# Turning normalised rows through memory and blocks on VectorE, and a written order for the last 13 attention steps

## The chip, the cores and the metric

The kernel runs on one core of one Trainium2 chip. The metric is the time of one execution on the device in microseconds (us), lower is better. It is the median of three runs, beside one execution that the hardware profiler recorded. All arithmetic is in float32.

## The reference, cut to what matters

An image x of 4 x 16 x 16 x 1024 passes two layers, three blocks in all, each of which adds to x: a convolution-like attention with relative positions (four heads), a causal attention (16 heads of 64, four sequences of 256 tokens), and a mixture of eight experts, of which each token takes those whose gate is at least 0.1.

```python
x = x + _L0_conv_ref(_gn(x), ...)                  # group norm, then lambda layer
t = _to_tokens(x)                                  # 4 x 256 tokens of 1024
t = t + _L1_attn_ref(_ln_t(t), W_attn, b_attn, W_proj, b_proj)
t = t + _L1_ffn_ref(_ln_t(t), gate_w, gate_b, expert_w, expert_b)

def _ln_t(v, eps=1e-5):
    m = jnp.mean(v, axis=-1, keepdims=True)
    s = jnp.var(v, axis=-1, keepdims=True)
    return (v - m) / jnp.sqrt(s + eps)
```

Both layer norms `_ln_t` are places of the change, and so is the end of `_L1_attn_ref`.

## The kernel before

**Shapes.** The 1024 tokens are eight tiles of 128 rows (NT = 8), the 1024 channels eight chunks of 128 (NC = 8). Image b holds tiles 2b and 2b + 1. A matrix product on PE wants the channels on the partitions, so that each tile of normalised rows has to be turned before it is used.

**Who sets the order.** Outside the blocks marked `tc.manual_schedule()` a scheduler orders the instructions of each engine when the kernel is built: by the order of the source and by its own costs, it takes what it holds to be ready. Each engine then works in that fixed order, SP's queue of transfers included. In a `manual_schedule` block the block's own instructions keep the order of the source on the engines named (without names, on all of them).

**End of the first block (lines 419 to 453).** For each tile, in the order 1, 3, 5, 7, 0, 2, 4, 6: two products `pc` (line 342) that VectorE adds into `s0`, four pairs of products `py` (443) that VectorE adds to x, and `layer_norm` (155 to 171): statistics on VectorE, the root on ACT, the normalised row on ACT (166), eight turnings on PE into PSUM (170), two copies on ACT into `ln1` (171). GpSimd then adds the output bias of the attention to x (452), and SP stores the tile in memory as `x_rows` (453).

**Attention.** `project_v` (499) makes V by seven products of blocks instead of eight (Strassen's way, as everywhere here): `sums_of_A` (149) and `sums_of_B` (479) are VectorE's sums for it. Queries and keys of a pair of heads come from seven units `project_qk(pair, n)` (532), each one product of half width. Then 32 steps follow, one for each pair of heads and image, the last eight with the pairs 6 and 7 in turn (673). A step's `scores` (573) are a product into the one PSUM tile `sc`, scale and mask on VectorE (593), row maxima (605), four exponentials on ACT (607), reciprocals (614) and four multiplications on GpSimd (617). The rows go out to memory (623) and come back in four reads (627), so that `turned` (630) has only to turn blocks of 32 x 32 on VectorE (632). `values` (638) of a step come three steps later (`lag`). `units` (675 to 681) says which units stand in which step, and `out_at` (682) which pieces of the output projection `project_out` (658) do: (tile, half of the channels), 16 matmuls by the profile's count. All of this is left to the scheduler. At step 27 SP loads x back from `x_rows`, eight tiles of 512 KB (694 to 697). The weights of the projection, two halves of 2 MB, are asked for with the first piece (660).

**Start of the experts (lines 708 to 1029).** The other ten pieces of the projection are cut into 20 halves. `after` (1003) places each tile's four stages behind numbered halves: `normalise` (853), `gate` (874), `place` (905), `enter` (941). `normalise` makes the row on VectorE (863), turns it on PE (845) with a copy on ACT (849) and one on VectorE (851), brings the row into quarters on ACT (867) and stores it in `rows` (871), from which the experts' rows are later gathered. Ahead of it SP is asked for the weights and the bias of expert 0 (984, 985).

Of the kernel before, what the change touches and what calls it, by code (L numbers as in the profile page):

```python
# [32 lines left out]
F32 = mybir.dt.float32  # L33
I32 = mybir.dt.int32
AF = mybir.ActivationFunctionType
# [32 lines left out]
def kernel(  # L68
# [86 lines left out]
    def layer_norm(ln, t, dst):  # L155
# [8 lines left out]
        less = small.tile([P, 1], F32, tag="ln_less", name=f"ln1_less{t}")  # L164
        nc.vector.scalar_tensor_tensor(less, mv[:, 0:1], -1.0, rstd, ALU.mult, ALU.mult)
        nc.scalar.activation(ln, xs[t], AF.Identity, bias=less, scale=rstd)  # L166
        for j in range(2):
            pt = tr(f"ln1_pt{t}_{j}")
            for c in range(4):
                nc.tensor.transpose(pt[:, ts(c, P)], ln[:, (4 * j + c) * P : (4 * j + c + 1) * P], ident)  # L170
            nc.scalar.copy(dst[:, 4 * j : 4 * j + 4, ts(t, P)], pt.rearrange("p (c n) -> p c n", c=4))


    with ExitStack() as layer0:
# [253 lines left out]
        ln1 = big_tile(1, "ln1")  # L428
        ln_rows = wpool.tile([P, 4, C], F32, tag="w", name="ln_rows")
        bp = ln_rows[:, 3, :]  # L430
        nc.gpsimd.dma_start(bp, b_proj.partition_broadcast(P))
        for i, (b, nt) in enumerate(tiles):
            if i == 0:
                content(b, nt)
            if i + 1 < NT:
                content(*tiles[i + 1])
            t = 2 * b + nt
            for hp in range(2):
                py = mm(f"py{t}_{hp}")
                for hl in range(2):  # L440
                    bh = b * HEADS0 + 2 * hp + hl
                    for mh in range(2):
                        nc.tensor.matmul(  # L443
                            py[:, ts(hl, M)],
                            s0[:, mh, ts(nt, S2), :, bh].rearrange("p i j -> p (i j)"),
                            v_T[:, mh, ts(b, M)],
                            start=(mh == 0),
                            stop=(mh == 1),
                        )
                nc.vector.tensor_add(xs[t][:, ts(hp, HALF)], xs[t][:, ts(hp, HALF)], py)  # L450
            layer_norm(ln_rows[:, i % 3, :], t, ln1)
            nc.gpsimd.tensor_add(xs[t], xs[t], bp)  # L452
            nc.sync.dma_start(x_rows[ts(t, P), :], xs[t])
# [3 lines left out]
    with ExitStack() as attention:  # L457
# [41 lines left out]
        def project_v(r):  # L499
# [3 lines left out]
            sums_of_A(*a, s1, s2, s4)  # L503
# [7 lines left out]
            for t in range(4):  # L511
                c11, c12, c21, c22 = homes(t)
                nc.scalar.copy(c22, one(t, 1, a11, b11))
                nc.vector.tensor_add(c11, one(t, 2, a12, b21), c22)
# [3 lines left out]
            for t in range(4):  # L518
                nc.scalar.copy(homes(t)[1], one(t, 3, s4, b22))
# [11 lines left out]

        def project_qk(pair, n):

            g, at = pair // 2, (pair % 2) * P
            if n == 1:
# [3 lines left out]
                S[pair] = s_pool.tile([P, 3, NC // 2, P], F32, tag="S", name=f"S_qk{pair}")  # L539
            a = [w_qk[g][:, 4 * j : 4 * j + 4, i * M + at : i * M + at + P] for i in range(2) for j in range(2)]  # L540
            a11, a12, s3, a22 = a
            s1, s2, s4 = (S[pair][:, i, :, :] for i in range(3))
            if n == 1:
                sums_of_A(*a, s1, s2, s4)
# [28 lines left out]
        def scores(pair, b):  # L573
# [29 lines left out]
            for qt in range(2):  # L603
                cols = slice(qt * P, qt * P + (qt + 1) * P)
                nc.vector.tensor_reduce(top[:, qt, :], s[:, :, cols], AX.X, ALU.max, negate=True)
                for h in range(2):
# [6 lines left out]
                    )  # L613
            nc.vector.reciprocal(total, total)  # L614
# [43 lines left out]
        def project_out(t, j, halfway=lambda: None):  # L658
            if not w_p:
                w_p.extend(w_tile(f"w_p{j}", W_projT[:, ts(j, HALF)]) for j in range(2))  # L660
            po = mm(f"po{t}_{j}")
            for c in range(NC):
                nc.tensor.matmul(po, y_T[:, c, ts(t, P)], w_p[j][:, c, :], start=(c == 0), stop=(c == NC - 1))  # L663
                if c == NC // 2 - 1:
                    halfway()
# [13 lines left out]
        units[22].remove((6, 5))  # L679
        units[23] = [(6, 5)]  # L680
# [668 lines left out]
```

## Time and profile before

| | |
|---|---|
| three runs | 1278.26, 1278.86 (median), 1281.36 us |
| profiled execution | 1278.4 us |
| its span on the core | 1276.6 us |
| mean granted clock of PE | 0.991 |
| first block with its layer norm, to the first product of V | 0 to 282.6 us |
| V, queries and keys, attention steps | 282.6 to 690.5 us |
| rest of the projection, gates and lists | 690.5 to 786 us |
| experts | 786 to 1276.6 us |

PE is TensorE's matmuls, PEld its weight loads, DVE is VectorE, ACT is ScalarE, POOL is GpSimd, and SP is the engine that issues most transfers. Lines such as L170 are lines of the kernel; a group's line gives what is written and read, the shape, the count, then the busy time in us and the mean of one in ns, and behind the second bar the idle time before it and what ended that. An instruction whose time overlaps its neighbour's shows more than it costs: of PE the distance from start to start is what counts. The granted clock of PE is given as a share of full speed. The profile counts two matmul instructions for each matmul of the source.

### The profile page before, as it was taken

The numbers are of one execution on the slowest core, as the hardware profiler recorded it, in microseconds if no ns is written. First come the engines' busy times: TensorE is split into PE (matmuls) and PEld (weight loads), VectorE is DVE, ScalarE is ACT, GpSimd is POOL, SyncE is SP. The second block draws the span as 40 slices with busy tenths as digits, with TensorE's granted clock in tenths as the row PEclk, the third lists the DMA queues.
The fourth block names the chain that finished last, engine by engine and source line by source line (L and its number), as shares of the span: only waits on it lengthen the run. The fifth ranks groups of instructions, "written<-read, shape, count | busy, mean of one in ns | idle before, by whom it ended". The sixth has DMA issues, their size and how long they took to land.

```text
span 1276.6 us, 12809 instructions
## 1 busy us (share of the span) xinstructions
PE 1248.8 (98%) x4646; PEld 657.0 (51%) x4646; DVE 694.6 (54%) x1297; ACT 221.6 (17%) x520; POOL 350.0 (27%) x423
## 2 busy tenths in 40 slices
PE   9999999999999999999889998999999999999997
PEld 5444895788884444444434544444344434433443
DVE  5784220566322666665545754755656665665642
ACT  3300111231000222222221322011111110111110
POOL 0000051230000222222210011554644544363520
PEclk9999999999999999999889998999999999999999
DMA  9020022612202535353744415274658375557442
GB/s 353 7 66 2 16 63 70 232 65 99 67 1 66 153 102 163 108 168 99 246 137 154 174 50 210 71 232 89 185 150 232 90 231 154 141 118 210 99 82 51
DMA packets 83605, 159.76 MB, mean 125 GB/s; under 512 B 8368, under 2 KB 39104, under 8 KB 83536
## 3 DMA queue, kind: packets, MB, share of 16 engines
q1 hardware_dynamic: 70704, 119.49, 27.3%
q0 software_dynamic: 12832, 39.39, 14.0%
q8 instruction: 38, 0.62, 0.2%
q14 instruction: 31, 0.25, 0.1%
HBM read 109.30 MB, written 45.35 MB: 121 GB/s over the span
## 4 chain that ended last, share of the span: by engine, by line
PE 75%; issue 13%; POOL 5%; DVE 3%; DMA 3%; ACT 0%; SPq 0%; POOLq 0%; ACTq 0%; DVEq 0%
PE p L1120 29%; PE po L663 7%; PE pq L259 7%; PE pv L492 7%; POOL s_q L617 5%; PE left L1162 3%; PE pT L378 3%; PE pqk L492 3%; PE py L443 2%; PE pk L321 2%; PE pc L342 2%; PE pv L403 2%; PE rest L1176 2%; PE last_pe L1274 1%; DMA s_rows<-s_q 1%
## 5 line engine op out<-in xcount | busy, mean ns | idle before, releaser
L735 POOL DMA_INDIRECT w_e_xg<-rows,gather x146 | 155.2, 1063 | 67.5 <-issue 41.7
L1120 PE MATMUL p<-w_e,A 128*128 128x512 f32 x368 | 163.2, 593 | 1.8 <-DVE slot L981 1.8
L617 POOL TENSOR_TENSOR s_q<-s_q,total 128x128 f32<-128x128 f32 (+1 forms) x128 | 65.3, 541 | 301.9 <-DVE total L614 301.9
L663 PE MATMUL po<-w_p,y_T 128*128 128x512 f32 x256 | 119.5, 613 | 0.0
L1120 PEld LDWEIGHTS p<-w_e,A 128*128 128x128 f32 x368 | 69.6, 190 | 90.4 <-issue 89.9
L1120 PE MATMUL p<-T,S 128*128 128x512 f32 x256 | 112.7, 593 | 0.0
L1126 ACT ACTIVATE y<-y,slot 128x512 f32<-128x512 f32 x64 | 46.0, 721 | 336.3 <-DVE y L1134 183.9
L763 POOL DMA_INDIRECT out_dram<-y,add x32 | 57.4, 1794 | 171.0 <-ACT y L1126 110.1
L259 PE MATMUL pq<-w_q,xn 128*128 128x512 f32 x224 | 99.6, 596 | 1.4 <-DVE q_s L263 1.1
L607 ACT ACTIVATE s_q<-s,top 128x256 f32<-128x256 f32 (+1 forms) x128 | 56.6, 443 | 182.6 <-issue 143.1
L492 PE MATMUL pqk<-ln,w_qk 128*128 128x512 f32 x192 | 86.0, 596 | 0.0
L1120 PEld LDWEIGHTS p<-T,S 128*128 128x128 f32 x256 | 48.6, 190 | 60.8 <-issue 60.7
L663 PEld LDWEIGHTS po<-w_p,y_T 128*128 128x128 f32 x256 | 47.5, 195 | 52.1 <-issue 51.9
L745 DVE STREAM_TRANSPOSE A<-w_e_xg 128x1024 f32<-128x1024 f32 x32 | 39.6, 1238 | 59.8 <-DMA w_e_xg<-rows,gather 56.6
L259 PEld LDWEIGHTS pq<-w_q,xn 128*128 128x128 f32 x224 | 41.8, 190 | 51.8 <-issue 47.4
L492 PE MATMUL pqk<-T,S_qk 128*128 128x512 f32 x128 | 58.3, 598 | 0.0
L492 PEld LDWEIGHTS pqk<-ln,w_qk 128*128 128x128 f32 x192 | 35.8, 190 | 42.7 <-issue 41.5
L1120 PE MATMUL p<-w_e,S 128*128 128x512 f32 x128 | 57.5, 592 | 0.0
L1120 PE MATMUL p<-T,A 128*128 128x512 f32 x128 | 57.5, 592 | 0.0
L492 PE MATMUL pv<-w_v,ln 128*128 128x256 f32 x192 | 43.4, 379 | 0.0
L1162 PE MATMUL left<-w_e,one 128*32 128x512 f32 x312 | 41.8, 593 | 0.0
L452 POOL TENSOR_TENSOR x_at<-x_at,ln_rows 128x1024 f32<-128x1024 f32 x8 | 19.4, 2429 | 76.6 <-ACT ln_rows L166 76.6
(265 smaller groups left out, 1781.0 us busy)
## 6 DMA issues: line engine op xcount, KB each, us to landing
w_e<-in_expert_w_dram SPq DMA_DIRECT2D x16, 2048.0 KB, 12.2
s_rows<-s_q SPq DMA_DIRECT2D x32, 384.0 KB, 2.5
s_rows<-s_rows SPq DMA_DIRECT2D x128, 96.0 KB, 2.4
w_qk<-in_W_attnT_dram SPq DMA_DIRECT2D x8, 1024.0 KB, 6.1
xn<-in_xT_dram SPq DMA_DIRECT2D x8, 512.0 KB, 5.8
x_at<-in_x_dram SPq DMA_DIRECT2D x8, 512.0 KB, 8.5
w_v<-in_W_attnT_dram SPq DMA_DIRECT2D x2, 2048.0 KB
x_rows<-x_at SPq DMA_DIRECT2D x8, 512.0 KB, 2.7
```

Of the source, the lines that this page charges most:

```text
L259: nc.tensor.matmul(pq, xn[:, c, ts(t, P)], w_q[kc][:, c, :], start=(c == 0), stop=(c == NC - 1))
L378: nc.tensor.matmul(out_T[:, g, :, :], window[:, kc, :, :].rearrange("p i j -> p (i j)"), q0[:, kc, first : first + n_i, nj, :], start=(kc ...
L492: nc.tensor.matmul(bank, stationary(c), moving(c), start=(c == 0), stop=(c == NC // 2 - 1))
L607: nc.scalar.activation(blocks(h, qt), s[:, h, cols].rearrange("p (b f i) -> p b f i", f=Q, i=32), AF.Exp, bias=top[:, qt, h : h + 1], accu ...
L617: nc.gpsimd.tensor_mul(blocks(h, qt), blocks(h, qt), total[:, qt, h : h + 1].unsqueeze(2).unsqueeze(3).to_broadcast([P, 1 + qt, Q, 32]),)
L663: nc.tensor.matmul(po, y_T[:, c, ts(t, P)], w_p[j][:, c, :], start=(c == 0), stop=(c == NC - 1))
L735: nc.gpsimd.indirect_dma_start(out=row[:, g, :], out_offset=None, in_=table[: (TOK - P) * Q, :] if e in SHORT else table, in_offset=bass.I ...
L745: nc.vector.transpose(row_T[:, :, :slots].rearrange("p c (g j) -> p g c j", j=32), row[:, : slots // 32, :].rearrange("p g (c i) -> p g c ...
L763: nc.gpsimd.indirect_dma_start(out=out[: TOK - P, :] if e in SHORT else out, out_offset=bass.IndirectOffsetOnAxis(ap=add[:slots, e, k : k ...
L1120: nc.tensor.matmul(bank, a[:, c, :], b[:, c, :], start=(c == 0), stop=(c == NC // 2 - 1))
L1126: nc.scalar.mul(y[i][:, ts(j, HALF)], y[i][:, ts(j, HALF)], slot[:, e, 1, 2 * pair + i : 2 * pair + i + 1])
L1162: nc.tensor.matmul(bank[ts(i, 32), :], stationary, w[of][j][:, c, :], start=(c == 0), stop=(c == NC - 1))
```

## The change

The change has four parts.

1. In the first layer norm ACT writes the normalised row by quarters, SP stores it in a scratch tile in memory and reads it back in four transfers, each into 32 partitions, and VectorE turns the 32 x 32 blocks. PE's turnings and ACT's copies go. SP's own order in this loop is that of the source, and GpSimd stores x. `sums_of_A` of V stands behind the last layer norm on VectorE, and the first products of V take the tiles in the order 1, 3, 0, 2.
2. Steps 22 to 34 of the attention (34 because the values lag by three) stand in a `manual_schedule` for all engines. Units come ahead of or behind a step's values and scores; in steps with a piece of the projection these stand before the last of its eight matmuls. The sums of pair 7 move to step 22. `scores` is cut in two: what ends with the exponentials, and `scored`, which has the rest from the reciprocal on.
3. x is loaded from GpSimd's queue, two tiles in each of the steps 28 to 31. The weights of the projection are asked for in steps 22 and 28, and the pieces' order becomes (0,0), (1,0), (0,1), (1,1), (2,0), (2,1).
4. In the second layer norm tiles 0 to 5 take the way of part 1, through `rows` itself; tiles 6 and 7 keep the old one. The stages' places in `after` move by up to two halves.

`quarters_of`, `turn` and `normalised` are defined ahead of `layer_norm`; `turn` is the old function of line 743, moved.

```diff
+    def normalised(row, of, mean, rstd):
+        less = small.tile([P, 1], F32, tag="ln_less", name="ln_less")
+        done = nc.vector.scalar_tensor_tensor(less, mean, -1.0, rstd, ALU.mult, ALU.mult)
+        nc.scalar.activation(
+            row.rearrange("p (f c i) -> p c f i", f=Q, c=NC),
+            of.rearrange("p (c f i) -> p c f i", c=NC, f=Q),
+            AF.Identity,
+            bias=less,
+            scale=rstd,
+        )
+        return done
...
+    def quarters_of(rows, home, name):
+
+        row = home.tile([P, Q, C // Q], F32, tag="xg", name=name)
+        for f in range(Q):
+            nc.sync.dma_start(row[ts(f, 32), :, :], rows[:, f, :].rearrange("(g j) c -> j g c", j=32))
+        return row
+
+    def turn(row_T, row, slots=P):
+
+        nc.vector.transpose(
+            row_T[:, :, :slots].rearrange("p c (g j) -> p g c j", j=32),
+            row[:, : slots // 32, :].rearrange("p g (c i) -> p g c i", c=NC),
+        )
+
+    def layer_norm(ln, t, dst, home, turns):
 
         stats = small.tile([P, 2, 6], F32, tag="ln_stats", name=f"ln1_stats{t}")
         for j in range(2):
@@ -161,14 +189,11 @@
         nc.vector.bn_aggr(mv, stats)
         rstd = small.tile([P, 1], F32, tag="ln_rstd", name=f"ln1_rstd{t}")
         inverse_root(rstd, mv[:, 1:2], EPS)
-        less = small.tile([P, 1], F32, tag="ln_less", name=f"ln1_less{t}")
-        nc.vector.scalar_tensor_tensor(less, mv[:, 0:1], -1.0, rstd, ALU.mult, ALU.mult)
-        nc.scalar.activation(ln, xs[t], AF.Identity, bias=less, scale=rstd)
-        for j in range(2):
-            pt = tr(f"ln1_pt{t}_{j}")
-            for c in range(4):
-                nc.tensor.transpose(pt[:, ts(c, P)], ln[:, (4 * j + c) * P : (4 * j + c + 1) * P], ident)
-            nc.scalar.copy(dst[:, 4 * j : 4 * j + 4, ts(t, P)], pt.rearrange("p (c n) -> p c n", c=4))
+        done = normalised(ln, xs[t], mv[:, 0:1], rstd)
+        rows = turns.tile([P, Q, C // Q], F32, tag="rows", name=f"ln1_rows{t}")
+        nc.sync.dma_start(rows.rearrange("n f c -> n (f c)"), ln)
+        turn(dst[:, :, ts(t, P)], quarters_of(rows, home, f"ln1_quarters{t}"))
+        return done
...
+        turns = layer0.enter_context(tc.tile_pool(name="turns0", bufs=3, space=bass.MemoryType.DRAM))
...
+        with tc.manual_schedule(engines={mybir.EngineType.SP}):
...
+                ln_done = layer_norm(ln_rows[:, i % 3, :], t, ln1, tpool, turns)
+                nc.gpsimd.tensor_add(xs[t], xs[t], bp)
+                nc.gpsimd.dma_start(x_rows[ts(t, P), :], xs[t])
...
-            sums_of_A(*a, s1, s2, s4)
+            with tc.issue_after(ln_done.ins):
+                sums_of_A(*a, s1, s2, s4)
...
-            for t in range(4):
+            in_time = (1, 3, 0, 2)
+            for t in in_time:
...
+        def sums_qk(pair):
+            S[pair] = s_pool.tile([P, 3, NC // 2, P], F32, tag="S", name=f"S_qk{pair}")
+            sums_of_A(*blocks_qk(pair), *(S[pair][:, i, :, :] for i in range(3)))
...
-        def project_out(t, j, halfway=lambda: None):
-            if not w_p:
-                w_p.extend(w_tile(f"w_p{j}", W_projT[:, ts(j, HALF)]) for j in range(2))
+        def project_out(t, j, between={}):
+
             po = mm(f"po{t}_{j}")
             for c in range(NC):
                 nc.tensor.matmul(po, y_T[:, c, ts(t, P)], w_p[j][:, c, :], start=(c == 0), stop=(c == NC - 1))
-                if c == NC // 2 - 1:
-                    halfway()
+                between.get(c, lambda: None)()
...
-        units[22].remove((6, 5))
-        units[23] = [(6, 5)]
-        units.update({24: [(7, 1), (7, 2), (7, 6)], 25: [(7, 7), (7, 4)], 26: [(6, 3), (7, 5)], 27: [(7, 3)]})
-        out_at = {28: (0, 0), 29: (1, 0), 30: (2, 0), 31: (0, 1), 32: (1, 1), 33: (2, 1)}
-        lag = 3
+        lag, written = 3, 22
         for n in order:
             project_qk(0, n)
-        soft = {}
-        for i in range(len(steps) + lag):
+        soft, turned_s = {}, {}
+        for i in range(written):
             if i >= lag:
-                s_T = turned(*steps[i - lag], soft.pop(i - lag))
+                turned_s[i - lag] = turned(*steps[i - lag], soft.pop(i - lag))
             for unit in units.get(i, ()):
                 project_qk(*unit)
-            if i == 27:
-                sums.close()
-                x_pool = pool(x_home, "xb", side="right")
-                xs = [x_pool.tile([P, C], F32, tag=f"x{t}", name=f"xb{t}") for t in range(NT)]
-                for t in range(NT):
-                    nc.sync.dma_start(xs[t], x_rows[ts(t, P), :])
             if i >= lag:
-                values(*steps[i - lag], s_T)
-            if i in out_at:
-                project_out(*out_at[i])
-            if i < len(steps):
-                soft[i] = scores(*steps[i])
+                values(*steps[i - lag], turned_s.pop(i - lag))
+            soft[i] = scored(*steps[i], *scores(*steps[i]))
+
+
+
+        units = {
+            22: ([(6, 4), (6, 5)], []),
+            23: ([], [(7, 1)]),
+            24: ([(7, 2)], [(7, 6)]),
+            25: ([(7, 7), (7, 4)], []),
+            26: ([(6, 3)], [(7, 5)]),
+            27: ([(7, 3)], []),
+        }
+        out_at = {28: (0, 0), 29: (1, 0), 30: (0, 1), 31: (1, 1), 32: (2, 0), 33: (2, 1)}
+        with tc.manual_schedule():
+            for i in range(written, len(steps) + lag):
+                if i == written:
+                    w_p.append(w_tile("w_p0", W_projT[:, :HALF]))
+                if i == 28:
+                    w_p.append(w_tile("w_p1", W_projT[:, HALF:]))
+                    sums.close()
+                    x_pool = pool(x_home, "xb", side="right")
+                    xs = [x_pool.tile([P, C], F32, tag=f"x{t}", name=f"xb{t}") for t in range(NT)]
+                if 28 <= i < 32:
+                    for t in range(2 * (i - 28), 2 * (i - 28) + 2):
+                        nc.gpsimd.dma_start(xs[t], x_rows[ts(t, P), :])
+                s_T = turned(*steps[i - lag], soft.pop(i - lag))
+                ahead, behind = units.get(i, ((), ()))
+                for unit in ahead:
+                    project_qk(*unit)
+
+                def values_and_scores():
+                    values(*steps[i - lag], s_T)
+                    return scores(*steps[i]) if i < len(steps) else None
+
+                made = []
+                if i in out_at:
+                    project_out(*out_at[i], {NC - 2: lambda: made.append(values_and_scores())})
+                else:
+                    made.append(values_and_scores())
+                if i == written:
+                    sums_qk(7)
+                for unit in behind:
+                    project_qk(*unit)
+                if made[0]:
+                    soft[i] = scored(*steps[i], *made[0])
...
-            nc.vector.tensor_scalar(row, xs[t], mv[:, 0:1], rstd, ALU.subtract, ALU.mult)
             row_T = l2w.tile([P, NC, P], F32, tag="row_T", name=f"row_T{t}", bufs=3)
-            transpose_rows(row, row_T, f"row{t}")
-            by_quarter = l2w.tile([P, Q, C // Q], F32, tag="xg", name=f"by_quarter{t}")
-            nc.scalar.copy(
-                by_quarter.rearrange("p f (c i) -> p c f i", c=NC),
-                row.rearrange("p (c f i) -> p c f i", c=NC, f=Q),
-            )
-            nc.sync.dma_start(rows[ts(t, P), :], by_quarter.rearrange("p f c -> p (f c)"))
+            if t < NT - 2:
+                normalised(row, xs[t], mv[:, 0:1], rstd)
+                nc.sync.dma_start(rows[ts(t, P), :], row)
+                turn(row_T, quarters_of(rows[ts(t, P), :].rearrange("n (f c) -> n f c", f=Q), l2w, f"quarters{t}"))
+            else:
+                nc.vector.tensor_scalar(row, xs[t], mv[:, 0:1], rstd, ALU.subtract, ALU.mult)
+                transpose_rows(row, row_T, f"row{t}")
+                by_quarter = l2w.tile([P, Q, C // Q], F32, tag="xg", name=f"by_quarter{t}")
+                nc.scalar.copy(
+                    by_quarter.rearrange("p f (c i) -> p c f i", c=NC),
+                    row.rearrange("p (c f i) -> p c f i", c=NC, f=Q),
+                )
+                nc.sync.dma_start(rows[ts(t, P), :], by_quarter.rearrange("p f c -> p (f c)"))
...
-            0: (0, 2, 4, 6),
-            1: (2, 4, 6, 8),
-            2: (4, 6, 8, 10),
-            3: (6, 8, 10, 12),
-            4: (9, 11, 13, 15),
-            5: (13, 14, 16, 17),
-            6: (17, 18, 21, 23),
+            0: (0, 3, 5, 7),
+            1: (2, 5, 7, 9),
+            2: (4, 7, 9, 11),
+            3: (6, 9, 11, 13),
+            4: (8, 11, 13, 15),
+            5: (12, 15, 17, 18),
+            6: (16, 18, 20, 22),
...
-            project_out(*piece, halfway)
+            project_out(*piece, {NC // 2 - 1: halfway})
```

## The prediction

> **What bounds the kernel now.** I read the page's table of busy times first, then the groups of PE, then a table of busy times by stretch, then who waited for whom, and last the timeline of SP's queue.
>
> ```profile
> PE 1248.8 (98%) x4646; PEld 657.0 (51%) x4646; DVE 694.6 (54%) x1297; ACT 221.6 (17%) x520; POOL 350.0 (27%) x423
> PE 75%; issue 13%; POOL 5%; DVE 3%; DMA 3%; ACT 0%; SPq 0%; POOLq 0%; ACTq 0%; DVEq 0%
> ```
>
> PE is busy 98% of the span, so only two things shorten this kernel: fewer instructions on PE, or the few places where PE stands or runs slowly. The groups of PE give the first:
>
> ```profile
> L170 PE MATMUL ln_pt<-ident,ln_rows 128*128 128x128 f32 x64 | 8.5, 275 | 1.4 <-ACT ln_rows L166 1.4
> L845 PE MATMUL row_pt<-ident,row 128*128 128x128 f32 x64 | 9.4, 295 | 4.9 <-DVE row L863 4.9
> ```
>
> These are the turnings on PE, 8 groups of 8 each. Their 275 ns overlap; from the start of a group to the start of what follows, the timeline has 0.87 to 0.93 us, so a group costs PE 0.9 us. The table by stretch gives the second (columns: stretch, its length, busy PE, PEld, DVE, ACT, POOL, granted clock, DMA share, GB/s):
>
> ```profile
> 578.89:624.70 45.81, 45.81 (x178) 21.56 (x176) 27.90 (x47) 11.86 (x49) 10.77 (x24) 1.00 0.44 141
> 624.70:632.40 7.70, 3.65 (x22) 1.96 (x21) 4.89 (x8) 3.28 (x15) 2.50 (x6) 0.80 0.79 245
> 632.40:690.49 58.09, 52.99 (x166) 23.81 (x164) 22.18 (x42) 7.72 (x29) 7.58 (x16) 0.91 0.41 140
> 690.49:697.19 6.70, 5.49 (x20) 2.75 (x19) 6.10 (x28) 0.91 (x1) 2.46 (x7) 1.00 0.92 260
> ```
>
> From 578.89 to 690.49 PE does exactly the last 13 steps of the attention. Up to 624.70 it is full. Then it is busy 3.65 of 7.70 us at a clock of 0.80, then 52.99 of 58.09 at 0.91. So the loss is in the last eight steps, as idle time and as matmuls at a slower clock after it. SP's queue in the timeline says why:
>
> ```profile
> 630.16 3.75 SPq L697 DMA_DIRECT2D xb<-x_rows  x6
> 634.01 1.44 SPq L623 DMA_DIRECT2D s_rows<-s_q  x2
> 643.11 3.93 SPq L627 DMA_DIRECT2D s_rows<-s_rows  x8
> ```
>
> Eight loads of x (512 KB each) go out between two steps' softmax rows. The rows written at 634.01 are read back only at 643.11, 9.1 us later, where 2.5 is the median of such a write. The scheduler's order adds two pairs of scores back to back that wait 3.0 and 1.6 us for VectorE's line 593, and a product with the values that waits 3.5 for s_T.
>
> **Part 1, the written order of the last 13 steps.** PE's work in it by the undisturbed groups of the same trace: 10 products pqk of 3.53 (two take 7.06), 6 products po of 7.06, 13 pa of 0.80, 10 sc of 0.85: 35.3 + 42.4 + 10.4 + 8.5 = 96.6 us. It took 690.49 - 578.89 = 111.6. **15.0 us** can go. Order and queue are the causes, and both change: x leaves SP for POOL, which in the tail does only four multiplications (1.90) per step, and scores stand one per step with 7 us of po between.
>
> What is late next? Each step's rows take from the end of its scores 5.7 us to the end of POOL's multiplication (scores end 624.79, POOL ends 630.46), 2.5 for the write, 1.7 to issue four reads, 2.4 for the last to land, 1.0 for VectorE to turn: 13.3. By the new order PE reaches the values that need them after 16.7 us at the least (step 31 to 34: 0.9 + 7.9 + 7.9) and some 20 or more elsewhere, so the three steps' lag covers it. Not so the second half of the projection's weights, w_p1 (2 MB). Before, SP issued it at 608.97. Now it stands on SP behind the reads of step 27, in an order that may not be changed. With S the end of that step's scores: issue at S + 5.7 + 2.5 + 1.7 = S + 9.9, and with the 8.4 us that w_p took, landed at S + 18.3. PE wants it after two steps of 7.06 + 0.80 + 0.85, at S + 17.4. That is 0.9 late alone; the x loads of two steps run beside it (four of 512 KB, of which eight queued together took 5.3 each) and may add 2 to 3. A wait of that length also costs slow matmuls behind it: the po group at 632.40 starts with one of 1.02 and three of 0.85 instead of 0.43, 1.85 more. So w_p1 costs 0 (issued ahead) to some 6 us; I take 3.5, by the bare 0.9 and most of the rest. The x of tile 0 lands by S + 5.7 + about 1 of issue + 5.3 = S + 12, where po is ready at S + 8.7. VectorE stands there, and behind it are step 28's reciprocal and step 29's turn, which PE wants at S + 14.7: 0 to 3, I take 0.5. The last step's turn stands on VectorE behind the last po's addition: 0 to 1.9, and products of tile 3 can fill it. Part 1: 15.0 - 4.0 = **11.0** (range 4 to 15).
>
> Here a rule speaks against the change. In the trace one queue held rows back for 9.1 us instead of 2.5. The Trainium skill ("DMA: Bandwidth & Descriptors", Rules for kernel authors) says that spreading transfers over SP, ACT and GpSimd does not help, as all run on the same 16 engines and interleave. By the rule alone these 6.6 us would stay and the sum below would be 16.0; by the row, what hurt was standing behind x in one queue, and they go.
>
> **Part 2, the first layer norm (lines 155 to 171).** Removed: 64 turnings on PE, 8 x 0.9 = 7.1 us, in a stretch (224 to 293) where PE has no other gap; the wait of 1.4 before the last of them; 16 copies on ACT (0.59). Together **8.5** on PE's path. Added for each tile: a write of 512 KB, four reads of 128 KB, and one turn on VectorE, 1.24 us (the same shape at line 745). The trip behind ACT's normalisation: 2.6 (rows of 512 KB) + 1.7 + 2.4 (s_rows reads of 96 KB) + 1.24 = 8.0. For the last tile PE has cover: the products of W_v that need other tiles are, by start-to-start times of 0.215, 8 products of 1.72 and three more, 18.9 us after the last py; the tile is ready some 4.2 (additions to normalised row) + 8.0 = 12.2 after it. sums_of_A, 6.4 us on VectorE which before stood in front of that tile's statistics, now stands behind them. The x_rows stores move to POOL, which is busy 2.4 of 7.9 us per tile. The danger is VectorE. Per tile it works 4.8 of 7.9 us; now 6.1 of 7.0. The turn stands in its in-order queue where the scheduler puts it, and if it stands before its rows have landed, everything behind it waits. Slack is 0.9 us per tile. Bounds: 0 to 8 x (8.0 - 1.24 - 0.9) = 47. I take 1.0, near the lower end: of the 70 turns in this trace (lines 632 and 745) one made PE wait for long, 3.5 us. Part 2: **7.5**.
>
> The second rule against the change: PE needs 0.9 us for a tile, the new way 8.0 of trip. The Trainium skill ("VectorE: DVE Perf Modes", Rules for kernel authors) advises TensorE for turning 128x128. By it this part would give nothing, and the sum would be 15.1; here PE is the full engine, and the row counts PE's time alone.
>
> **Part 3, the second layer norm (lines 853 to 872).** Six of eight tiles lose their turnings on PE: 6 x 0.9 = 5.4; the wait of 1.2 at 695 before the first goes with them (VectorE's L863 stood behind set-up work). Together **6.6**. On VectorE 0.81 + 0.69 per tile give way to 1.24. Tiles 6 and 7 keep theirs, and so the stall of 3.7 before the last one stays. What is late next is tile 0's gate:
>
> ```profile
> 690.92 1.52 SPq L119 DMA_DIRECT2D w_e<-in_expert_w_dram  x2
> 692.53 4.92 SPq L728 DMA_DIRECT2D w_e_bias<-in_expert_b_dram  x1
> 697.54 2.99 SPq L871 DMA_DIRECT2D rows<-by_quarter  x2
> ```
>
> The rows go out behind 4.5 MB of expert weights; ACT's line 867 waited 4.7 us, until 711.1, for them. Before, nothing on PE needed that write. Now tile 0's four reads, landing and turn follow: 711.1 + 1.7 + 2.4 + 1.2 = 716.4, while the gate's new place is four half pieces behind 690.5, at 704.6. If PE is made to stand there, it costs 11.8; if the scheduler puts more of the projection first, 0. That ACT wait shows it misjudging this very transfer by about 4.7. I take 2.5. Part 3: **4.1**.
>
> **Sum.** 11.0 + 7.5 + 4.1 = 22.6. The profiled execution took 1278.4 (span 1276.6, 1.8 around it), 0.5 under the median of 1278.86. 1278.4 - 22.6 = 1255.8: **1256 us**.
>
> **Rivals.**
> - All covers hold: 15.0 + 8.5 + 6.6 = 30.1 go, 1248. For it: lags of 16.7 us and more against 13.3. Chance 0.15.
> - The tail exchanges its waits: w_p1 6, x 3, the last turn 1.9, one more slow restart 1.85, so 12 of 15.0 stay. 30.1 - 12 - 1 - 2.5 = 14.6, 1264. Against it: SP is free of x. Chance 0.15.
> - The gate waits: 11.8 and a slow restart 1.85, 13.7. 30.1 - 4 - 1 - 13.7 = 11.4, 1267. Chance 0.10. With the case above, 1275 to 1276 (no change): 0.04.
> - Slower: VectorE held by turns in the first layer norm. With a wait w per tile it costs 8 x (w - 0.9); against the 23.6 of the other terms it decides from w = 3.9. At w = 5.5 it is 36.8, so 1292. For it: 87% load on an in-order queue; against it: three PSUM buffers let PE run ahead. Chance 0.08.
> - The forecast, 1251 to 1260 by itself: 0.48.
>
> A measurement of this kernel can tell 0.3%, 3.8 us, from no change. Faster by more: 0.48 + 0.15 + 0.15 + 0.10 = 0.88; within: 0.04; slower: 0.08. The range of 1246 to 1268 reaches from a little under the first rival to the third and leaves out 0.12.
>
> **What would show it.** Right: no L170 on PE and 16 of L845; the 13 steps within 101 us at a clock near 1.00; line 443's last product to the first of line 492's without a gap. Wrong: PE waiting for w_p1 at the third po by over 6 us; the gate's parts (line 879) waiting on VectorE's turn; VectorE idle behind DMA between 230 and 290. The prediction fails if one of these holds over 10 us.

## The result, and the profile after

The changed kernel takes **1286.12 us** (median of five runs, 1284.67 to 1286.33) against 1278.86: ratio 1.005, 95% interval 1.0035 to 1.0064. It is slower by 0.5%, where 1256 us was forecast. The profiled execution took 1286.1 us, its span is 1284.2.

First the two lines of the page that answer to those of before: busy times by engine, and the chain that ended last by engine.

```profile
PE 1239.6 (97%) x4534; PEld 647.6 (50%) x4534; DVE 706.7 (55%) x1305; ACT 208.7 (16%) x496; POOL 359.7 (28%) x439
PE 45%; DMA 2%; DVE 2%; POOL 1%; issue 1%; ACT 0%; SPq 0%; POOLq 0%; DVEq 0%; ACTq 0%
```

The work did leave PE: 112 matmul instructions fewer (64 of the first layer norm, 48 of the second), 9.2 us less busy time. Yet the span grew by 7.6, so PE stands about 17 us longer. Of the two groups of turnings one is gone and the other has 16 left:

```profile
L905 PE MATMUL row_pt<-ident,row 128*128 128x128 f32 x16 | 3.0, 353 | 1.3 <-DVE row L929 1.3
```

Who waited for whom, on PE (us in total, times, longest):

```profile
PE pv L519 <- DVE ln L178: 10.1, 2, 8.2
PE pa L683 <- DVE s_T L671: 8.5, 3, 5.8
PE po L701 <- DMA w_p<-in_W_projT_dram: 5.8, 1, 5.8
PE lists L1008 <- DVE g_keep L961: 3.3, 1, 3.3
```

Before, PE waited once for `s_T`, 3.5 us, and for none of the other three. One of the four sits in the first layer norm, two in the written steps, one in the second layer norm. The table by stretch shows what they cost, with the columns of the prediction's table:

```profile
277.44:300.00 22.56, 12.49 (x49) 10.08 (x48) 15.50 (x20) 3.68 (x7) 7.02 (x5) 0.85 0.55 168
592.30:606.00 13.70, 7.94 (x34) 4.57 (x33) 9.34 (x17) 3.73 (x16) 2.06 (x5) 0.75 0.29 88
655.90:665.00 9.10, 3.31 (x5) 1.17 (x4) 4.03 (x7) 1.86 (x8) 2.96 (x6) 0.81 0.98 360
784.40:812.33 27.93, 22.84 (x122) 12.45 (x123) 17.48 (x81) 6.78 (x9) 9.88 (x11) 0.82 0.73 245
```

The stretches begin with the first product of V, at the values of step 23, at the third piece of the projection, and behind the last piece. In each PE is idle for 5 to 10 us, and its mean clock is below 1.

The same points of the program in both traces, in us from the start of the span:

| first start of | before | after | shift |
|---|---|---|---|
| products of V | 282.63 | 277.44 | -5.2 |
| products of queries and keys | 382.73 | 388.24 | +5.5 |
| step 22 | 578.89 | 584.40 | +5.5 |
| end of the attention's last values | 690.49 | 701.18 | +10.7 |
| experts' `p` (L1120, now L1185) | 803.94 | 812.33 | +8.4 |
| end | 1276.6 | 1284.2 | +7.6 |

At 701.18 PE has already done 0.86 us of a later piece of the projection. So the first layer norm costs 5.5 net, the 13 written steps 4.3 (115.9 instead of 111.6), and the second layer norm gives 1.4. The last 0.8 us are gained in the experts, whose code is the same in both kernels (471.9 us from `p` to the end, 472.7 before).

SP's queue, for the forecast's fence on x:

```profile
649.39 0.40 SPq L119 DMA_DIRECT2D w_p<-in_W_projT_dram  x1
653.02 0.34 SPq L662 DMA_DIRECT2D s_rows<-s_q  x1
663.27 1.74 SPq L666 DMA_DIRECT2D s_rows<-s_rows  x4
```

x is no longer here, and the rows written at 653.02 are still read back only 10.2 us later. The same stretch by the columns of the table, first the 9.1 us in which the rows of before were held (the prediction's fence), then these 10.2:

```profile
634.00:643.10 9.10, 9.10 (x29) 3.97 (x28) 2.64 (x4) 0.00 (x0) 1.10 (x3) 0.88 0.96 364
653.02:663.22 10.20, 4.41 (x21) 1.97 (x20) 4.90 (x8) 1.86 (x8) 4.01 (x8) 0.91 0.98 351
```

The last column but one is alike: the DMA engines were busy at a share of 0.96 and 0.98, whichever queue had issued x.

### The profile page after: what moved, and what is told of

Same layout as the page of the kernel before. It is cut to its first block, busy times and chain, and to the rows that moved or that the text cites. A ratio compares the mean times of both kernels' runs of the same rounds, so it can differ in the third digit from the quotient of the medians.

```text
span 1284.2 us, 12711 instructions
## 1 busy us (share of the span) xinstructions
PE 1239.6 (97%) x4534; PEld 647.6 (50%) x4534; DVE 706.7 (55%) x1305; ACT 208.7 (16%) x496; POOL 359.7 (28%) x439
## 3 DMA queue, kind: packets, MB, share of 16 engines
q0 software_dynamic: 15136, 47.78, 15.9%
## 4 chain that ended last, share of the span: by engine, by line
PE 45%; DMA 2%; DVE 2%; POOL 1%; issue 1%; ACT 0%; SPq 0%; POOLq 0%; DVEq 0%; ACTq 0%
PE p L1185 29%; PE po L701 8%; PE left L1227 3%; PE rest L1241 2%; PE last_pe L1339 1%; DMA w_p<-in_W_projT_dram 1%; POOL w_e_xg L802 1%; DMA out_dram<-dense_ye,token_i 1%; PE pqk L519 1%; PE pa L683 1%; DMA w_e_xg<-rows,gather 0%; POOL entry L997 0%; PE sc L614 0%; PE parts L944 0%; DVE one L989 0%
## 5 line engine op out<-in xcount | busy, mean ns | idle before, releaser
L1185 PE MATMUL p<-w_e,A 128*128 128x512 f32 x368 | 163.2, 593 | 1.8 <-DVE slot L1046 1.8
L1185 PEld LDWEIGHTS p<-w_e,A 128*128 128x128 f32 x368 | 69.6, 190 | 90.4 <-issue 89.7
L1185 PE MATMUL p<-T,S 128*128 128x512 f32 x256 | 112.7, 592 | 0.0
L1185 PEld LDWEIGHTS p<-T,S 128*128 128x128 f32 x256 | 48.6, 190 | 60.8 <-issue 60.8
L1185 PE MATMUL p<-T,A 128*128 128x512 f32 x128 | 57.5, 592 | 0.0
L1185 PE MATMUL p<-w_e,S 128*128 128x512 f32 x128 | 57.5, 592 | 0.0
L519 PE MATMUL pv<-w_v,ln 128*128 128x256 f32 x192 | 45.3, 390 | 10.1 <-DVE ln L178 10.1
L519 PEld LDWEIGHTS pv<-w_v,ln 128*128 128x128 f32 x192 | 37.5, 196 | 16.2 <-issue 10.8
```

Of the source, the lines that this page charges most:

```text
L519: nc.tensor.matmul(bank, stationary(c), moving(c), start=(c == 0), stop=(c == NC // 2 - 1))
L1185: nc.tensor.matmul(bank, a[:, c, :], b[:, c, :], start=(c == 0), stop=(c == NC // 2 - 1))
```

## The experiments

Theory A: the three parts act independently, and each loses at a place of its own, where an order written by hand or by the scheduler puts one instruction behind another that isn't ready. Rivals: the parts lean on each other; or the way through memory is in itself too long. Every kernel was compared with runs of the kernel before on the same chip (medians there 1279.4 to 1280.5); the ratios below are to these. The changed kernel ran beside 1278.86, so a difference of medians to it comes out too small by some 0.6 to 1.7 us.

### Each part alone

`only_ln1` has the changed first layer norm with V's order, `only_tail` the written steps with x from GpSimd, `only_ln2` the changed second layer norm with its stages. The rest of each is the kernel before. One place of each edit:

```diff
# only_ln1
+        turn(dst[:, :, ts(t, P)], quarters_of(rows, home, f"ln1_quarters{t}"))
# only_tail
+        with tc.manual_schedule():
+            for i in range(written, len(steps) + lag):
# only_ln2
+            if t < NT - 2:
+                normalised(row, xs[t], mv[:, 0:1], rstd)
```

> Before, with the first layer norm's part alone (rows turned through memory, SP in written order, x stored by GpSimd, sums of V behind the last layer norm). Theory A (each part carries its own waits): PE loses the 64 turnings, 7.1 us and the wait of 1.4, and gains the waits for VectorE's turn that the changed kernel shows between 284 and 312, 14 us in all; so slower by 5 to 6, about 1284.5. Theory B (the parts hurt each other through queues and the order of the whole): this part alone is faster, by up to 8.5, 1270 to 1277.

> Before, with the written order of steps 22 to 34 and x from GpSimd's queue alone. Theory A: the 15 us of lost time go, and in their place come 5.9 and a slow restart of 2.2 before the values of step 23, 1.3 before those of step 27, 6.0 and a slow restart of 3.0 before the third po, 1.8 before the last values, 20 in all; so slower by 4 to 5, about 1283. Theory B: without the later parts' transfers beside it w_p1 lands in time, and it is faster, 1265 to 1275.

> Before, with the second layer norm's part and the moved stages alone. Theory A: 5.4 us of turnings and 1.2 of wait go, some 4 to 5 come back at the end, where the gates of tiles 5 and 6 now stand in VectorE's queue ahead of the last tile's row; faster by 1 to 3, about 1277. Theory B: the end is late because everything ahead is late; alone this part gains 5 or more, 1274 or less.

Measured: `only_ln1` 1284.32, ratio 1.0037 (1.0023 to 1.0051). `only_tail` 1285.70, 1.0049 (1.0032 to 1.0066). `only_ln2` 1276.95, 0.9978 (0.9968 to 0.9988). Against their 1280.0 that is +4.3, +5.7 (+3 was expected) and -3.1, together +6.9; the whole change costs 7.3. Two of the three cost time by themselves, and by the medians the parts add up. That they do so to 0.4 us is in part luck, since the intervals alone allow some 3. In the traces the shift of the experts' `p` is +4.5, +4.6 and -3.3, together +5.7, where the whole change has +8.4: the second layer norm gives 3.3 alone and 1.4 in company. Behind `p` the three take 474.2 to 475.8 us where the changed kernel takes 471.9 (more on this under the combinations). So theory A holds to about 3 us.

### The written steps: two places

At step 28 w_p1 is asked for at 649.39 and lands at 662.27; PE wants it at 656.5. `wp26` asks two steps earlier:

```diff
+                if i == 26:
+                    w_p.append(w_tile("w_p1", W_projT[:, HALF:]))
                 if i == 28:
-                    w_p.append(w_tile("w_p1", W_projT[:, HALF:]))
                     sums.close()
```

`units23` gives step 23 two products ahead of its values, where it had none:

```diff
-            22: ([(6, 4), (6, 5)], []),
-            23: ([], [(7, 1)]),
+            22: ([(6, 4)], []),
+            23: ([(6, 5), (7, 1)], []),
```

`tail_mended` has both.

> The changed kernel with w_p1 asked for at step 26 instead of step 28, nothing else. If the written place of that load alone makes the third po wait: 6.0 and the slow restart of 3.0 go, 1277. If x on GpSimd's queue, sharing the transfers, is what makes it late: it lands hardly earlier in relation to its use, under 3 us gained, 1283 or more.

> The changed kernel with units (6,5) and (7,1) ahead of the values of step 23, nothing else. If VectorE's written order (scores, four sums of pair 7, reciprocal, then the turn) without PE's work beside it makes the wait at step 23: 5.9 and the slow restart of 2.2 go, 1278. If the rows land late: the wait stays behind the two units, 1283 or more.

> The changed kernel with two places of the written order moved: units (6,5) and (7,1) stand ahead of the values of step 23 instead of at step 22 and behind, and w_p1 is asked for at step 26 instead of 28. Theory A: the waits of 5.9 + 2.2 and 6.0 + 3.0 go, 17 less, about 1269; small waits before steps 27 and 34 stay. Theory B: what is late is the rows' trip through memory, and the wait moves to another step; 1280 or more.

Measured: `wp26` 1277.08, 0.9977 (0.9967 to 0.9987). `units23` 1279.01, 0.9992 (0.9983 to 1.0002). `tail_mended` 1271.89, 0.9937 (0.992 to 0.9953). Moving one line gives 9 us and moving two products 7; both together 14.2, where 17 was expected. Up to `p` the three are 9.1, 8.4 and 15.9 ahead of the changed kernel; behind it the last two lose 1.9 again. What PE waits for in `tail_mended`:

```profile
PE pv L519 <- DVE ln L178: 10.0, 2, 8.2
PE pa L683 <- DVE s_T L671: 3.9, 3, 1.7
PE lists L1009 <- DVE g_keep L962: 3.3, 1, 3.3
```

The wait for w_p is gone, that for `s_T` is down from 8.5 to 3.9, and the first layer norm's is untouched.

### What holds the turn of step 23

VectorE does the four sums of pair 7 between step 22's scores and step 23's turn. That looked like the cause. `sums23` moves only them, behind the turn:

```diff
                 s_T = turned(*steps[i - lag], soft.pop(i - lag))
+                if i == written + 1:
+                    sums_qk(7)
...
-                if i == written:
-                    sums_qk(7)
```

> The changed kernel with the four sums of pair 7 moved on VectorE from the end of step 22 to behind the turn of step 23, no product moved. Theory A (the turn of step 23 stands in VectorE's written order behind the reciprocal of step 22's scores, which waits for ScalarE's exponentials until about 596.8 whatever the sums do; the step lacks products between scores and values): the turn comes 1.1 us earlier, 1286.1 - 1 = 1285, range 1284 to 1286. Rival B (the four sums are what holds the turn): 2.7 us and the slow restart go, 1282 to 1283.5.

Measured: 1283.89, 1.0041 (1.0028 to 1.0054), a little under A's range and 0.4 above B's: the time does not decide. The trace does. VectorE in `sums23`:

```profile
594.17 1.01 DVE L640 TENSOR_REDUCE top<-s 128x2 f32<-128x256 f32 x2
596.63 0.18 DVE L653 RECIPROCAL total<-total 128x4 f32<-128x4 f32 x1 [1.45 <-ACT s_q L642]
596.83 0.98 DVE L671 STREAM_TRANSPOSE s_T<-s_rows 128x768 f32<-128x768 f32 x1
```

The same turn in the changed kernel:

```profile
597.95 0.95 DVE L671 STREAM_TRANSPOSE s_T<-s_rows 128x768 f32<-128x768 f32 x1
```

Without the sums VectorE stands idle for 1.45 us and waits for ACT's exponentials, since the reciprocal of step 22 precedes the turn of step 23. The turn begins at 596.83 instead of 597.95, and PE's longest wait falls from 5.8 to 4.8. The sums filled most of a wait that was there anyway. The rows had landed at 579.1; what was missing was work on PE between scores and values, as `units23` shows, where the wait of 5.8 us is gone.

### The first layer norm

In the changed kernel, PE beside VectorE at the first products of V:

```profile
277.44 7.07 PE L519 MATMUL pv<-w_v,ln 128*128 128x256 f32 x32
292.75 5.42 PE L519 MATMUL pv<-w_v,ln 128*128 128x256 f32 x16 [8.24 <-DVE ln L178]
```

```profile
280.76 2.21 DVE L159 SCALAR_TENSOR_TENSOR ln_less<-ln_mv,ln_rstd 128x1 f32<-128x1 f32 x1
282.90 1.21 DVE L150 TENSOR_TENSOR s_v<-w_v 128x1024 f32<-128x1024 f32 x1
...
285.50 3.35 DVE L153 TENSOR_TENSOR w_v<-w_v 128x1024 f32<-128x1024 f32 x1
288.78 1.23 DVE L178 STREAM_TRANSPOSE ln<-ln_quarters 128x1024 f32<-128x1024 f32 x1
...
291.38 1.22 DVE L178 STREAM_TRANSPOSE ln<-ln_quarters 128x1024 f32<-128x1024 f32 x1
```

The quarters of the tiles 7 and 0 had landed at 269.8 and 281.1. Their turns stand behind the statistics of the last tile and behind `sums_of_A`. With two buffers for quarters, SP's reads of tile 2 wait for the turn of tile 7 (290.04), and SP's written order puts the store of tile 4, whose row ACT had finished at 280.4, behind them (291.87).

`ln1_four` gives four buffers and leaves the orders alone. `ln1_lag` has three buffers and a written order for SP and VectorE: in iteration i store i, turn i-2, read i-1. `ln1_written` writes the order for PE and ACT too, goes on to V's first 12 products, reads i-1 ahead of the store of i, and puts the sums of W_v one by one between V's. Behind the chain of tile i it turns tile i-2, not i-1 as the expectation has it, and it asks for the first half of W_v ahead of the loop and for the second behind those 12 products.

```diff
# ln1_four
-        row = home.tile([P, Q, C // Q], F32, tag="xg", name=name)
+        row = home.tile([P, Q, C // Q], F32, tag="xg", name=name, bufs=bufs)
# ln1_lag
-        with tc.manual_schedule(engines={mybir.EngineType.SP}):
+        with tc.manual_schedule(engines={mybir.EngineType.SP, mybir.EngineType.DVE}):
...
+                stored.append((t, rows_t))
+                if back:
+                    turn_back()
+                if i:
+                    fetch_back()
# ln1_written
+        by_hand = {mybir.EngineType.SP, mybir.EngineType.DVE, mybir.EngineType.PE, mybir.EngineType.Activation}
+        written.enter_context(tc.manual_schedule(engines=by_hand))
...
                 nc.vector.tensor_add(c11, one(t, 2, a12, b21), c22)
+                if r == 0:
+                    sums.pop(0)()
+            if r == 0:
+                turn_back()
```

> The changed kernel with four buffers instead of two for the quarters of the first layer norm. If SP's wait for a buffer, with the next tile's store behind it, makes the waits at V: the later ones (2.0 and 1.8) go and the first one shrinks only by little, since it is the turn of an earlier tile that stands late on VectorE; 1281 to 1284. If two buffers were the whole cause: 1272 to 1275.

> The changed kernel with the first layer norm's trip in three written lags on SP and VectorE: in round i tile i is stored, tile i-1 read back and tile i-2 turned behind the statistics of tile i; three buffers for the quarters. If late turns on VectorE and the queue behind them (a read that waits for a turn's buffer, and the next store behind that read) make the waits of 14 us at V: these go and 1286 becomes 1272 to 1274. If the trip itself is too long: waits of 5 or more stay before V's products, 1278 or more.

> The changed kernel with the first layer norm and the first 12 products of V in one written order on SyncE, VectorE, ScalarE and TensorE: rows of tile i-1 read back ahead of the store of tile i, the turn of tile i-1 behind the chain of tile i, the sums of W_v one at a time between the sums of V, the last turn behind them; three buffers. Theory A (the way through memory can be covered, what stands in the way is only where the scheduler puts the turns and the sums): the 12.5 us that V's products wait go, 1286.1 - 12 = 1274, range 1272 to 1276. Rival B (the last tile's trip of 13.3 us cannot be covered by what is left for TensorE, or the written order of VectorE holds py): at most what the lags gave, 1280 to 1283.

Measured: `ln1_four` 1286.04, 1.0046 (1.003 to 1.0063): no gain, against my expectation, and PE still waits 10.0 for the turns. The late turns, not the buffers, set the time. `ln1_lag` 1282.74, 1.0023 (1.0013 to 1.0032): 3.4 of the expected 12 to 14. Its trace says why:

```profile
283.17 0.42 DVE L560 TENSOR_TENSOR v<-pv,v 128x256 f32<-128x256 f32 x1 [4.50 <-ACT v L559]
283.51 1.23 DVE L178 STREAM_TRANSPOSE ln<-ln_quarters 128x1024 f32<-128x1024 f32 x1
```

V's first sum lies outside the written block, so the scheduler put it on VectorE ahead of the last tile's chain. VectorE waited 4.5 us for it, and with it the additions of the last `py`, which had ended at 280.8. `ln1_written` took 1275.08, 0.996 (0.9947 to 0.9974): 11.0 less than the changed kernel, as A said. PE in its trace:

```profile
271.12 7.25 PE L485 MATMUL py<-v_T,s 128*128 128x256 f32 x32
278.20 13.98 PE L539 MATMUL pv<-w_v,ln 128*128 128x256 f32 x64
293.80 6.50 PE L539 MATMUL pv<-s_v,ln 128*128 128x256 f32 x29 [1.62 <-DVE s_v L553]
```

The eight products of the first four tiles run without a gap, and the remaining wait of 1.62 is for a sum of W_v, not for a turn. The last quarters land at 293.6, 15.4 after the last `py`; VectorE has turned them at 296.27, and PE doesn't wait for them. So the way through memory can be covered; as the scheduler ordered it, it was not.

### Combinations

`no_ln1_mended` is `tail_mended` with the first layer norm of before, `all_written` is `ln1_written` with the two mends of the steps. `tile5_mended` is `tail_mended` with one more tile of the second layer norm turned on PE, and `all_tile5` has everything:

```diff
-            if t < NT - 2:
+            if t < NT - 3:
```

> The kernel before's first layer norm (turned on TensorE), with the written steps 22 to 34, w_p1 at step 26, (6,5) and (7,1) ahead of the values in step 23, and the changed second layer norm. Theory A (the parts add up): 1271.9 - 5.5 = 1266.4, range 1265 to 1268. Rival B (the parts of the change lean on each other): 1270 or more.

> The changed kernel with all three mends: first layer norm in the written order, w_p1 at step 26, (6,5) and (7,1) ahead of the values in step 23. Theory A: 1271.9 - 12 = 1260, range 1258 to 1262. Rival B: 1266 to 1269, no better than with the layer norm of before.

> The changed kernel with the mends of the written steps (1271.9) and, in the second layer norm, tile 5 turned on TensorE as tiles 6 and 7 are. Theory A (tile 5's way through memory pushes its gate into the gates of 6 and 7, and they into the chain of the last row, which came 7.8 us after the last product): 0.9 us of turnings come back, 2 to 4 go: 1269 to 1271. Rival B (the gates crowd because they begin late, whichever engine turns tile 5): 1272.5 to 1273.

> The changed kernel with all four mends: written first layer norm, w_p1 at step 26, (6,5) and (7,1) ahead of the values in step 23, tile 5 turned on TensorE in the second layer norm. Theory A (the four waits are the whole difference between the forecast and the result, and they are independent): 1259.6 - 3 = 1256.5, range 1255 to 1258. Rival B (with the earlier ones gone, the wait at the end of the second layer norm is covered otherwise): 1259 or more.

Measured: `no_ln1_mended` 1265.88, 0.9885 (0.987 to 0.99). `all_written` **1259.58**, 0.984 (0.9827 to 0.9854). Both are theory A's numbers. `all_written` is faster than both kernels of the study: 21 us under before on its chip, 26.5 under the change.

`tile5_mended` 1269.16, 0.9919 (0.9906 to 0.9933), 2.7 less than `tail_mended` by the medians, with intervals that overlap. In the changed kernel VectorE makes the last row (L929) at 791.81, 7.6 us after the last addition to x (784.24), behind the gates of two tiles. In `tile5_mended` (L930) it does so at 774.16, 3.8 us after the addition at 770.37. The experts' `p` begins 3.0 earlier than in `tail_mended` (793.43 against 796.40). The stretch from the last matmul of the projection to `p` shows it, in before, the changed kernel, `tail_mended` and `tile5_mended`:

```profile
779.43:803.94 24.51, 20.83 (x85) 10.67 (x85) 14.75 (x61) 5.78 (x8) 8.63 (x9) 0.86 0.77 277
784.04:812.33 28.29, 22.86 (x122) 12.46 (x123) 17.80 (x83) 6.78 (x9) 9.88 (x11) 0.82 0.72 242
768.57:796.40 27.83, 22.39 (x123) 12.41 (x124) 17.80 (x83) 6.77 (x9) 9.85 (x11) 0.82 0.73 246
770.23:793.43 23.20, 19.08 (x84) 9.80 (x84) 13.55 (x52) 6.36 (x8) 8.65 (x9) 0.93 0.83 294
```

With tile 5 on PE some 40 matmul instructions of gates and lists no longer stand in it, and the clock is higher. The wait of 3.3 us for the lists stays, though.

`all_tile5` took 1259.62, 0.984 (0.9827 to 0.9853): the same as `all_written`, so A's 1256.5 was missed. Rival B's number (1259 or more) came, but not by its reason: in the profiles `p` begins 2.3 earlier (782.05 against 784.37), and the end comes only 0.9 earlier. What eats the rest is the clock behind `p`. The same stretch of the experts, 22.5 us behind the start of `p`, in `all_written` and then in `all_tile5`:

```profile
806.90:810.30 3.40, 3.40 (x9) 1.52 (x8) 3.33 (x6) 0.43 (x1) 0.00 (x0) 1.00 0.00 0
804.60:808.00 3.40, 3.40 (x5) 1.34 (x4) 2.99 (x5) 0.31 (x1) 0.00 (x0) 0.51 0.00 0
```

In `all_tile5` PE runs 3.4 us at half the clock there, and from `p` to the end it is busy 465.57 us instead of 463.87 for the same instructions. Ten of the sixteen profiles have such a stretch at this place, among them the three parts alone, `units23` and `tail_mended`; before, the changed kernel, `wp26`, `ln1_lag`, `ln1_written` and `all_written` have none. All sixteen have a wait of 1.8 us at this place (`p` for `slot`), so what decides is not shown, nor whether it is the kernel or the single execution. Two of the five runs of `all_tile5` were at 1257.0 and 1257.3, the others at 1259.6 to 1259.9. A difference of some 2 us between two of these kernels can come from this alone.

## Why the prediction was wrong

**What bounds the kernel** held: PE's own work fell as counted, and the sum of the parts was the right form.

**Part 1** was to give 11.0 and cost 4.3. Two steps failed. The first is "the three steps' lag covers it": the trip of 13.3 us is covered, but I compared it only with PE's time and not with VectorE's written order. In step 23 nothing stands on PE between scores and values, and VectorE's turn comes behind the reciprocal of the step before. That cost 5.8 us and about 2.2 of slow matmuls behind it. The second is the size of the term for w_p1: 3.5 taken, 6 the upper end. PE waited 5.8 and then ran seven matmuls at about 0.85 instead of 0.43, 3.0 more. Issue and use came within 0.6 us of where I had put them; the transfer took 12.9 us from issue to landing, not 8.4 with 2 to 3 for the x beside it. In `wp26`, ahead of x, it took 8.35. With both mended (`all_written`) the 13 steps take 100.3 us, 11.3 less than before: the 11.0 was there to be had. The last turn's wait, put at 0 because products of tile 3 could fill it, is 1.7 in both.

The **rule on spreading transfers** (the Trainium skill, "DMA: Bandwidth & Descriptors", Rules for kernel authors) was set aside by a row, wrongly. The page gives it for bandwidth, and bandwidth was what ran out. I read the 9.1 us of before as standing behind x in one queue, but the DMA engines were busy at a share of 0.96 then. With x on GpSimd's queue and w_p1 alone on SP's, rows were held 10.2 us, and from 648 to 663 the share was 1.00. (Those rows made PE wait nowhere; w_p1 did.) It is the moment of the transfers that counts: in `wp26`, with the same two queues, the rows' writes land 2.3 to 5.6 us after issue and no piece waits for w_p1. No run moves x to the other queue and nothing else, so what the queue is worth by itself is not shown.

**Part 2** was to give 7.5 and cost 5.5. The step that failed is the choice between its bounds of 0 and 47: "I take 1.0", because turns elsewhere had rarely made PE wait. PE waited 10.1 for turns and 1.6 for sums. The rival had named VectorE's order as the danger but with the sign reversed: turns did not stand too early and hold others up, those of the first six tiles stood 4 to 19 us after their quarters had landed, behind work that PE didn't need yet. "PE has cover" was right, as `ln1_written` shows: there the stretch from the last `py` to the queries and keys goes without a wait for a turn, and the first product of these comes at 377.18, 5.6 before the 382.73 of before (6.6 in `all_written`). The trip of the last tile was 18.1 with its turn (15.4 to the landing), not 12.2, and just under the 18.9 of cover. The second rule that I had set against the change, to leave the turning to TensorE, came nearer to the changed kernel than my sum did; it holds for the scheduler's order, not for the written one.

**Part 3** was to give 4.1 and gave 1.4. The step that failed is "what is late next is tile 0's gate", with 2.5 for it and nothing for the gates behind. Its place four half pieces behind was no danger: the scheduler put the projection first (the 0 of my bounds), and gate 0's product stands at 730.56 without a wait. Up to the last matmul of the projection the part gave 5.2 of its 6.6. What I left out is what then comes late: all gates shift, those of tiles 5 and 6 crowd into the last row's chain, and from that matmul to `p` PE needs 28.3 us instead of 24.5. With tile 5 back on PE the part gives 4.6 (from the end of the attention to `p`: 113.45 before, 108.8 in `tile5_mended`). Of the two waits in that stretch, 3.3 for the lists and 1.3 for the row, only the second gets shorter by it; why the lists are late stays open.

**The rivals.** The tail's exchange came closest: 19.3 of wait and slow matmuls stand where 15.0 were. (Its four terms add up to 12.75, not to the 12 that I took.) The slower case had VectorE in the first layer norm as its mechanism; its direction was right and its queue position wrong. I gave 0.08 to slower because I let the parts fail one at a time; three failed together, each at a mild price. Nor did one of the three signs of failure that I had named come: w_p1 made PE wait 5.8 and not over 6, no gate waited for a turn, and VectorE did not stand idle behind a DMA between 230 and 290. All three ask when data land; what I had not asked is what stands in front of the consumer when they have landed.

## What to carry to other kernels

When an order is written by hand, check for each wait both sides: when the data land, and what stands in front of the consumer in its own engine's queue. A written block is only as good as its edges: instructions outside it are slipped in between (4.5 us here), so write it through to the first consumer that must not wait. Ask for a weight early enough that its transfer doesn't meet the others: here another moment helped (9 us for one moved line), while on another queue the rows were held as long as before.

## What the runs showed of the hardware

- VectorE instructions beside a GpSimd addition can take many times as long. L159 (128x1) took 2.21 us instead of 0.14 beside the first of these, L153 (128x1024) 3.35 instead of 1.16 beside the second:

```profile
280.61 2.35 POOL L479 TENSOR_TENSOR x_at<-x_at,ln_rows 128x1024 f32<-128x1024 f32 x1
284.42 3.36 POOL L479 TENSOR_TENSOR x_at<-x_at,ln_rows 128x1024 f32<-128x1024 f32 x1 [0.58 <-ACT ln_rows L160]
```

L159 ended with the addition (282.97 and 282.96), L153 1.07 us behind it (288.85 and 287.78), about its own length. The Trainium skill ("SBUF — State Buffer", Terms) states that the two engines share a port pair which one holds for a whole instruction while the other blocks; these rows fit that. In `ln1_written` the four sums of W_v, run when GpSimd had finished, took 1.20 to 1.21 each.
- After a wait of 5.8 us seven matmuls in a row ran at half speed (0.85 us from start to start instead of 0.43), so the wait cost half as much again: 8.8 us.
- At the same wait of 1.8 us (`p` for `slot`) the clock was halved for 3.4 us or more in ten profiles and not in six; it cost PE 1.7 us in `all_tile5` (3.4 us at half the clock) and 2.9 in `only_ln1` (6.8 us).
